# The stage ahead of the layers in written order: x loaded first, block steps pipelined, sort and first lists beside the last blocks

## The chip, the cores and the metric

The kernel runs on 1 core of one Trainium2 chip. The metric is device time in microseconds of one execution of the whole kernel, from launch to the last output. Beside it there is the trace of one profiled execution: the start and length of every instruction on each engine (PE is the TensorE matmul, PEld its weight load, DVE is VectorE, ACT is ScalarE, POOL is GpSimd, SP is SyncE, which here only issues DMAs) and of every DMA.

## The reference, cut to what matters

A graph of N = 3327 nodes is given by a matrix `adj` of int32 zeros and ones (about 16 neighbours a row), with features `x` of 3327 x 256 in float32. Layer 0 is a one-headed graph attention; the three layers after it are graph transformer layers with 8 heads, each node attending to its neighbours only.

```python
# layer 0
h = x @ Wt.T + bt                                     # 3327 x 64
s = leaky_relu(h @ Wa.T + ba, 0.2)                    # one score for each row
w = softmax(where(adj > 0, s, -9e15), axis=1)
y = x + (w @ h) @ Wp.T + bp
x = gamma * (y - mean(y)) * rsqrt(var(y) + 1e-5) + beta

# layers 1 to 3, weights of their own
q, k, v = split(layer_norm(x, g1, be1) @ w_qkv)       # 8 heads of 32
attn = softmax(where(adj != 0, q @ k.T * 32 ** -0.5, -inf))
x = x + (attn @ v) @ w_proj + b_proj
x = x + gelu(layer_norm(x, g2, be2) @ w1 + b1) @ w2 + b2   # w1 256 x 1024
```

As the score belongs to the row, all neighbours of a row get one weight and all others another; so layer 0 needs for each row the sum of `h` over the neighbours, the degree, and the sum of `h` over all nodes.

## The kernel before, in words

The nodes lie in `NB` = 26 blocks of 128 rows (the last has 127). There are two stages.

**The stage ahead of the layers (L172 to L468)** is layer 0 and all that the layers need. It stands in the scheduling of the tile framework: the program text says what depends on what, and the framework's scheduler sets the order of the instructions on each engine. In the order of the text:

- Small loads on ACT's queue: 15 columns of gains (`cols`, L188), the layer 0 weights `wt_raw`, `wp_raw` and a row of six vectors (L202), then `x` in 9 pieces (L209, L212) into `x0`, then `w_qkv` of layer 1 (`load_wq`, L90). The row is spread over the 128 partitions by matmuls with ones (L227).
- `h` (L258 to L274): per group of four blocks x is transposed on PE (L265), copied by DVE (L266), multiplied by Wt (`ph`, L270) and given its bias. When all of `h` is there, DVE splits it into three bf16 parts, `hs` (L279 to L283), with a column of ones behind them; 52 passes on PE sum `h` over all nodes (`phsum`, L288); L293 to L297 make the scores.
- The block loop (L401 to L432). Of a block: 1.66 MB of `adj` come on SP's queue into one of three `a32` buffers; ACT casts them to bf16 `abf` (L406); PE transposes its 26 tiles (L412) and ACT takes the sign of eight at a time into `aT` (L413); PE multiplies these with `hs` and sums into `pa` (L417), neighbour sums and degree together; ACT copies `pa` to `acc` (L424). For the neighbour lists DVE multiplies `abf` by column numbers (L421) and takes the eight largest of each of 13 segments of 256 columns (L423); the 104 candidates and the degree go to `node_dr` in DRAM (L426).
- After every fourth block: `count` (L304) makes the degree's one-hot `oh` and each node's rank among equal degrees, with matmuls; `finish` (L323) makes the softmax weights from the degree, mixes the sums, transposes (`nT`), multiplies with Wp (`pp`), adds to `x0`, and normalises: `moments` (L110: DVE statistics, then a power on POOL, L120), then on DVE L382 (subtract mean, times gamma) and L383 (times deviation, plus beta). Then a second norm for layer 1: statistics, `nmu` (DVE, L127), `xn` (ACT, L131), transposes and `hT` (ACT, L143), and `qkv_rows` (L157): k and v as `pk` (L161), q as `pq`, both copied by ACT, written on SP's queue to `kv_dr` and, with x, to `node_dr` (L388 to L391).
- Behind the loop the sort by degree (L435 to L468): the rank in all, from it one-hot matrices and 26 matmuls, and in the end `perm`, the node numbers sorted by degree.

**The layers (L471 to L781)** stand in an order written out by hand (`tc.manual_schedule()`, L779): each engine takes its instructions in the order in which the text issues them. Blocks are now 128 sorted nodes, in the order of `ORDER`. `node_rows` (L492) fetches a block's rows of `node_dr` with an indirect DMA of POOL by `perm`; `node_list` (L499) makes from the candidates the neighbours' numbers `idx`, the bias of empty places, and two counts (`found`), and ACT copies x to `x_sb`. Three blocks' rows are fetched ahead; the list of a block is made when the loop gets there. `gather` fetches k and v rows of up to four neighbours of each node with four indirect DMAs (L640, tiles `sl`); scores and weighted sums run on DVE (L651, L652, L684), the sums over neighbours on PE (L687), and `tail` (L546 to L589) does projection, norms, the feed-forward part, and k, v and q of the next layer. Layers 2 and 3 load their q rows on SP's queue (`load_q`); the `w_qkv` of the next layer is loaded at the start of each layer on ACT's queue (L90). A branch behind all, `general` (L812), computes the layers with full rows should a list not have held all neighbours; it is not entered with these inputs.

Of the kernel before, what the change touches and what calls it, by code (L numbers as in the profile page):

```python
# [36 lines left out]


# [11 lines left out]
NODES = 5  # L50
FH = FF // P // 2
# [6 lines left out]
def kernel(ctx: ExitStack, tc: tile.TileContext, ins, out: bass.AP):  # L58
# [21 lines left out]
    node_dr = dram.tile([NP, NODE], FP, name="node")  # L80
    q_dr = {L: dram.tile([P, NB, D], FP, name=f"q{L}") for L in LAYERS[1:]}
# [3 lines left out]
    pv = const.tile([P, 3, 16], FP, name="pv")  # L85
    wq_pool = ctx.enter_context(tc.tile_pool(name="wq", bufs=1))

    def load_wq(L):
        t = wq_pool.tile([P, 2, 3 * D], FP, tag="wq", name=f"wq{L}")
        nc.scalar.dma_start(t, wt(L, "w_qkv").rearrange("(c p) n -> p c n", p=P))  # L90
        return t


    brow = const.tile([6, D], FP, name="brow")
    for L in LAYERS:
        for k, name in enumerate(("b_proj", "b2")):
            r = 2 * (L - 1) + k
            nc.scalar.dma_start(brow[r:r + 1, :], wt(L, name)[None, :])
    b3 = const.tile([6, 3, D], BF, name="b3")
    for k in range(3):  # L100
        nc.vector.tensor_copy(b3[:, k, :], brow)
        if k < 2:
            nc.vector.tensor_sub(brow, brow, b3[:, k, :])
    bsum = const.tile([3, 6, D], BF, name="bsum")
    for k in range(3):
        nc.scalar.dma_start(bsum[k:k + 1, :, :], b3[:, k, :])
    ones3 = const.tile([3, P], BF, name="ones3")
    nc.vector.memset(ones3, 1.0)

# [60 lines left out]


    with ExitStack() as st:  # L172
# [4 lines left out]
        ps_g = st.enter_context(tc.tile_pool(name="ps_g", bufs=3, space=PSUM))  # L177
# [3 lines left out]

        cols = l0.tile([P, P], FP, name="cols")
        nc.vector.memset(cols, 0.0)
        for L in LAYERS:
            o = 16 * (L - 1)
            for k, name in ((0, "g1"), (2, "be1"), (4, "g2"), (6, "be2"), (8, "b1")):
                n = wt(L, name).shape[0] // P
                nc.scalar.dma_start(cols[o + k:o + k + n, :], wt(L, name).rearrange("(c p) -> c p", p=P))  # L188
        pt = big("pt_cols")
        nc.tensor.transpose(pt[:, :P], cols, ident)  # L190
        nc.vector.tensor_copy(pv, pt[:, :48].rearrange("p (l k) -> p l k", l=3))

        wt_raw = l0.tile([H0, D], FP, name="wt_raw")
        nc.scalar.dma_start(wt_raw, ins["L0_gnn_Wt"])
        wp_raw = l0.tile([P, 2, H0], FP, name="wp_raw")
        nc.scalar.dma_start(wp_raw, ins["L0_gnn_Wp"].rearrange("(c p) h -> p c h", p=P))
        nrow = 3 * D + 2 * H0 + 1
        row = l0.tile([1, nrow], FP, name="row")
        o = 0
        for name, n in (("gamma", D), ("beta", D), ("bp", D), ("bt", H0), ("Wa", H0), ("ba", 1)):  # L200
            src = ins[f"L0_gnn_{name}"]
            nc.scalar.dma_start(row[:, o:o + n], src if len(src.shape) == 2 else src[None, :])  # L202
            o += n

        x0 = l0.tile([P, NB, D], FP, name="x0")
        nc.vector.memset(x0[96:P, NB - 1, :], 0.0)
        for g, blocks in enumerate(GROUPS):
            full = [i for i in blocks if ROWS[i] == P]
            nc.scalar.dma_start(x0[:, full[0]:full[0] + len(full), :],  # L209
                                ins["x"][full[0] * P:(full[-1] + 1) * P, :].rearrange("(k p) d -> p k d", p=P))  # L210
        for p0, p1 in ((0, 112), (112, LAST)):
            nc.scalar.dma_start(x0[p0:p1, NB - 1, :], ins["x"][(NB - 1) * P + p0:(NB - 1) * P + p1, :])  # L212

        wtT = l0.tile([P, 2, H0], FP, name="wtT")
        wpT = l0.tile([H0, D], FP, name="wpT")
        for c in range(2):
            pt = big(f"pt_w{c}")
            nc.tensor.transpose(pt[:, :H0], wt_raw[:, c * P:(c + 1) * P], ident[:H0, :H0])
            nc.tensor.transpose(pt[:H0, P:2 * P], wp_raw[:, c, :], ident)
            nc.vector.tensor_copy(wtT[:, c, :], pt[:, :H0])  # L220
            nc.vector.tensor_copy(wpT[:, c * P:(c + 1) * P], pt[:H0, P:2 * P])

        rowb = l0.tile([P, nrow], FP, name="rowb")
        for c0 in range(0, nrow, 512):
            cw = min(512, nrow - c0)
            pb = big(f"pb_row{c0}")
            nc.tensor.matmul(pb[:, :cw], ones[0:1, :], row[:, c0:c0 + cw], start=True, stop=True)  # L227
            nc.scalar.copy(rowb[:, c0:c0 + cw], pb[:, :cw])
        gam_b, bet_b, bp_b = (rowb[:, k * D:(k + 1) * D] for k in range(3))
        bt_b = rowb[:, 3 * D:3 * D + H0]  # L230
        wa_b = rowb[:, 3 * D + H0:3 * D + 2 * H0]
        ba_b = rowb[:, nrow - 1:nrow]

# [21 lines left out]
        for s in range(1, SEGS):  # L255
            nc.gpsimd.tensor_copy(num[:, s, :], num[:, 0, :])

        h_sb = l0.tile([P, NB, H0], FP, name="h_sb")  # L258
        for g, blocks in enumerate(GROUPS):
            n = len(blocks)  # L260
# [43 lines left out]
        def count(g, acc):  # L304
# [8 lines left out]
            for j in range(n):  # L313
                nc.tensor.matmul(pc[:, j, :], tri, oh[:, b0 + j, :], start=True, stop=False)
                for m in range(j):
                    nc.tensor.matmul(pc[:, j, :], ones_bf, oh[:, b0 + m, :], start=False, stop=False)
# [655 lines left out]
```

## Time and profile before

| | |
|---|---|
| median of 4 runs | 3103.21 us (3098.36 to 3104.7) |
| profiled execution | 3107.19 us |
| its span, first to last instruction | 3105.4 us |
| mean granted TensorE clock | 0.741 of full speed |
| busy, share of the span | PE 58%, PEld 44%, DVE 57%, ACT 25%, POOL 47% |
| the stage ahead of the layers | from 0 to about 390 us |
| first instruction of x's loads | 24.49 us |
| last first-layer q row issued | 371.61 us |
| `perm` | 384.83 us |
| first gather of layer 1 | 397.12 us |

All times inside the trace count from the span's start. In a row of the order of time there stand: start, length, engine, line, operation, output <- inputs, shapes, how many like it follow in one go, and in brackets the idle time of the engine before it and whom it waited for. An engine name with q (ACTq, SPq) marks the issue of a DMA on that engine's queue; its length is the time to the landing. A table of stretches gives for each the length and the sum of the instructions' time on PE, PEld, DVE, ACT and POOL with their number, then the granted clock of PE, the share of time the DMA engines are busy, and GB/s.

### The profile page before, as it was taken

Reading aid. Unit: us, or ns where it says so; the run is one execution under the profiler, and the core shown is the slowest. Engines: PE = TensorE matmul, PEld = TensorE weight load, DVE = VectorE, ACT = ScalarE, POOL = GpSimd, SP = SyncE. Lnnn points to the kernel's source line nnn. Section 1 sums busy time; section 2 is a strip of 40 time slices with the busy share of each in tenths; the row PEclk is TensorE's granted clock in tenths of the full one; section 3 lists DMA queues with packets and bytes.
Section 4 is the critical chain, followed back from the end, with each engine's and each line's share of the span. In section 5 each row is a group of like instructions: output and inputs, shape, how many; then the busy total and the mean of one; then the engine's idle time right before and its main releaser. Section 6 shows DMA issues by size and latency. Waiting matters only on the chain. (4 is left out here: it accounts for less than half of the span.)

```text
span 3105.4 us, 25607 instructions
## 1 busy us (share of the span) xinstructions
PE 1793.7 (58%) x8349; PEld 1370.7 (44%) x8349; DVE 1778.1 (57%) x3203; ACT 768.0 (25%) x1420; POOL 1445.8 (47%) x1632
## 2 busy tenths in 40 slices
PE   6778405566655556825657665746634555445556
PEld 5555204444534444614445443435433444334445
DVE  4988546665556666426655655655264556554563
ACT  2877201222212122301322211211301212111112
POOL 0112164554555555254555655553354455555561
PEclk9999756777767777856878776767856777666767
DMA  5664164554545455164555555553354445544551
GB/s 189 210 216 163 67 195 124 145 158 131 162 144 150 140 157 149 51 208 116 149 155 146 162 162 149 153 158 100 122 157 136 118 135 158 162 142 142 147 154 29
DMA packets 154567, 451.22 MB, mean 145 GB/s; under 512 B 30575, under 2 KB 57849, under 8 KB 151097
## 3 DMA queue, kind: packets, MB, share of 16 engines
q0 software_dynamic: 111168, 363.51, 40.6%
q1 hardware_dynamic: 38462, 80.03, 7.6%
q10 hardware_dynamic: 4794, 5.94, 0.6%
q8 instruction: 69, 1.13, 0.2%
q14 instruction: 74, 0.61, 0.1%
HBM read 410.48 MB, written 38.88 MB: 145 GB/s over the span
## 5 line engine op out<-in xcount | busy, mean ns | idle before, releaser
L640 POOL DMA_INDIRECT sl<-kv,idx x1290 | 1233.2, 956 | 447.7 <-issue 373.7
L687 PE MATMUL po<-ident,sl 128*128 128x128 f32 x2580 | 492.4, 354 | 691.5 <-DVE sl L684 495.1
L687 PEld LDWEIGHTS po<-ident,sl 128*128 128x128 f32 x2580 | 411.7, 185 | 758.0 <-DVE sl L684 530.9
L651 DVE TENSOR_TENSOR sl<-sl,qp 128x1024 f32<-128x1024 f32 (+1 forms) x354 | 396.8, 1121 | 338.9 <-ACT qp L634 196.1
L580 PE MATMUL pd<-w,gT 128*128 128x256 f32 x1248 | 357.9, 447 | 217.8 <-ACT gT L571 157.8
L567 PE MATMUL pu<-fT,w 128*128 128x256 f32 (+1 forms) x1344 | 357.2, 410 | 120.0 <-issue 86.5
L652 DVE TENSOR_REDUCE sc<-sl 128x32 f32<-128x1024 f32 (+1 forms) x354 | 398.2, 1125 | 14.9 <-DVE sl L651 3.0
L580 PEld LDWEIGHTS pd<-w,gT 128*128 128x128 f32 x1248 | 276.1, 228 | 288.0 <-ACT gT L571 172.2
L684 DVE TENSOR_TENSOR sl<-sl,qp 128x1024 f32<-128x1024 f32 (+1 forms) x354 | 389.1, 1119 | 2.6
L567 PEld LDWEIGHTS pu<-fT,w 128*128 128x128 f32 x1344 | 265.4, 214 | 180.1 <-issue 109.9
L571 ACT ACTIVATE gT<-pu,pv 128x256 f32<-128x256 f32 (+1 forms) x336 | 135.1, 457 | 551.2 <-remote 316.5
L585 DVE TENSOR_TENSOR x_sb<-x_sb,pd 128x512 f32<-128x512 f32 (+1 forms) x42 | 27.3, 649 | 406.7 <-PE pd L580 394.0
L548 DVE TENSOR_TENSOR x_sb<-x_sb,pp 128x512 f32<-128x512 f32 (+1 forms) x42 | 27.3, 650 | 387.7 <-PE pp L546 365.3
L161 PE MATMUL pk<-wq,hT 128*128 128x512 f32 x312 | 193.8, 754 | 93.0 <-ACT hT L143 90.8
L120 POOL TENSOR_TENSOR rsig_f<-rsig_f,mhalf 128x2 f32<-128x2 f32 (+1 forms) x42 | 29.2, 695 | 305.9 <-DVE rsig_f L119 288.2
L602 POOL DMA_INDIRECT kv<-kvr,perm x52 | 52.4, 1007 | 240.4 <-ACT kvr L163 184.0
L693 ACT COPY oT<-po 128x256 f32<-128x256 f32 x78 | 29.1, 373 | 492.7 <-remote 252.7
L131 ACT ACTIVATE xn_f<-x_sb,nmu_f,rsig_f 128x256 f32<-128x256 f32 x78 | 43.4, 594 | 404.3 <-DVE nmu_f L127 258.5
L161 PEld LDWEIGHTS pk<-wq,hT 128*128 128x128 f32 x312 | 68.6, 239 | 153.0 <-ACT hT L143 99.3
L423 DVE MAX8 cand<-abf 128x8 f32<-128x256 bf16 x338 | 119.2, 412 | 0.0
L120 POOL TENSOR_TENSOR rsig_h<-rsig_h,mhalf 128x2 f32<-128x2 f32 (+1 forms) x28 | 19.5, 695 | 200.4 <-DVE rsig_h L119 200.4
L546 PE MATMUL pp<-w_proj,oT 128*128 128x256 f32 x312 | 95.7, 458 | 10.4 <-ACT oT L693 10.0
(217 smaller groups left out, 2021.7 us busy)
## 6 DMA issues: line engine op xcount, KB each, us to landing
a<-in_adj_dram SPq DMA_DIRECT2D x25, 1663.5 KB
sl<-kv,idx POOLq DMA_INDIRECT x1290
kv<-kvr SPq DMA_DIRECT2D x26, 256.0 KB
q<-qr SPq DMA_DIRECT2D x52, 128.0 KB
q<-q SPq DMA_DIRECT2D x52, 128.0 KB
w<-in_L_gnn_w_dram SPq DMA_DIRECT2D x6, 1024.0 KB
node<-x SPq DMA_DIRECT2D x26, 128.0 KB
node<-qr SPq DMA_DIRECT2D x26, 128.0 KB
```

The source lines that it names most:

```text
L161: nc.tensor.matmul(pk, hT[:, c, :], wq[:, c, D:], start=(c == 0), stop=(c == 1))
L423: nc.vector.max(out=cand[:, 8 * m:8 * m + 8], in_=ab3[:, m, :])
L546: nc.tensor.matmul(pp[:, j, :], oT[:, c, j * P:(j + 1) * P], w["w_proj"][:, c, :], start=False, stop=(c == 1 and j == n - 1))
L567: nc.tensor.matmul(pu[:, a, :n * P], w["w1"][:, c, f * P:(f + 1) * P], fT[:, c, :n * P], start=(c == 0), stop=(c == 1))
L571: nc.scalar.activation(gT[:, f0 + a, :n * P], pu[:, a, :n * P], AF.Gelu_apprx_tanh, bias=pv[:, L - 1, 8 + f:9 + f])
L580: nc.tensor.matmul(pd[:, j, :], gT[:, f, j * P:(j + 1) * P], w["w2"][:, h * FH + f, :], start=False, stop=(h == 1 and f == FH - 1 and j == ...
L602: nc.gpsimd.indirect_dma_start(out=kv_dr[L + 1][:, :], out_offset=bass.IndirectOffsetOnAxis(ap=perm[:, b:b + 1], axis=0), in_=kv, in_offse ...
L640: nc.gpsimd.indirect_dma_start(out=t[:, k - a, :], out_offset=None, in_=kv_dr[self.L][:, :], in_offset=bass.IndirectOffsetOnAxis(ap=idx[:, ...
L651: nc.vector.tensor_mul(kq, kq, self.qp[:, None, :D].to_broadcast([P, n, D]))
L652: nc.vector.tensor_reduce(self.sc[:, a:z, :], kq.rearrange("p s (h d) -> p s h d", h=HEADS), AX.X, ALU.add)
L684: nc.vector.tensor_mul(vv, vv, self.pw[:, a:z, :, None].to_broadcast([P, n, HEADS, HD]))
L687: nc.tensor.matmul(self.po[:, c, :], t[:, k, D + c * P:D + (c + 1) * P], ident, is_transpose=True, start=False, stop=(a + k == self.S - 1 ...
```

## The change

It rewrites the stage ahead of the layers, and keeps what it computes. The whole stage now stands in `tc.manual_schedule()`, so that every engine takes its instructions in the order of the text.

- *Loads.* On ACT's queue only the layer 0 weights and the row; on SP's queue x first, then three blocks of `adj`, then the columns, biases and `w_qkv`. `load_wq` issues on SP's queue in all layers.
- *h.* In 13 pairs of blocks instead of 7 groups; the copy of the transposed x moves from DVE to ACT; the split into three parts is made per two pairs, beside the following ones. The casts of blocks 0 and 1 come at the end of this.
- *Block loop.* Iteration i issues, in turns of up to eight tiles, transposes and signs of block i and the sums `pa` of block i-1; then the copies and writes of block i-1, the cast of block i+2 and the load of block i+4; one step of `finish`; the candidates of block i; one step of `finish` again (two of them in the last three blocks).
- *finish* is a generator which takes in `count`; each `yield` is a step's end. Several groups can be under way, each of them moved by a step at a time. The groups are `FIN`: five of four blocks, then 3, 2 and 1. The first norm is computed by ACT (x times deviation, minus mean times deviation) and by POOL (times gamma, plus beta, two blocks at a time).
- *Sort and first lists.* `order` is a generator too, started behind the last group's first step. It ends with the lists of the first three sorted blocks (`EARLY`), whose candidates come with `node_cand` from a table of their own, `cand_dr`; so each candidate row is written twice. `idx`, `bias`, `found` and the list's scratch tiles move to a pool that lives through both stages, and `segb` is filled at the start.
- *Layer 1* fetches the whole rows of the first three blocks (`node_rows`), copies their x, and makes lists from the fourth block on.

The diff, cut to its core:

```diff
+FIN = [list(range(a, z)) for a, z in ((0, 4), (4, 8), (8, 12), (12, 16), (16, 20), (20, 23), (23, 25), (25, 26))]
+EARLY = 3
...
+    cand_dr = dram.tile([NP, CAND + 1], FP, name="cand")
+    lists = ctx.enter_context(tc.tile_pool(name="lists", bufs=1))
...
     def load_wq(L):
-        nc.scalar.dma_start(t, wt(L, "w_qkv").rearrange("(c p) n -> p c n", p=P))
+        nc.sync.dma_start(t, wt(L, "w_qkv").rearrange("(c p) n -> p c n", p=P))
...
+    def node_cand(b):
+        nodes_[b] = lists.tile([P, NODE], FP, tag="node", bufs=NODES, name=f"node_{b}")
+        nc.gpsimd.indirect_dma_start(
+            out=nodes_[b][:, 2 * D:], out_offset=None, in_=cand_dr[:, :],
+            in_offset=bass.IndirectOffsetOnAxis(ap=perm[:, b:b + 1], axis=0))
...
-    with ExitStack() as st:
+    with ExitStack() as st, tc.manual_schedule():
-        ps_g = st.enter_context(tc.tile_pool(name="ps_g", bufs=3, space=PSUM))
+        ps_g = st.enter_context(tc.tile_pool(name="ps_g", bufs=4, space=PSUM))
+        nc.scalar.dma_start(wt_raw, ins["L0_gnn_Wt"])
+        nc.scalar.dma_start(wp_raw, ins["L0_gnn_Wp"].rearrange("(c p) h -> p c h", p=P))
...
+            nc.scalar.dma_start(row[:, o:o + n], src if len(src.shape) == 2 else src[None, :])
...
+            nc.sync.dma_start(x0[:, full[0]:full[0] + len(full), :],
+                              ins["x"][full[0] * P:(full[-1] + 1) * P, :].rearrange("(k p) d -> p k d", p=P))
...
+        load(0)
+        load(1)
+        load(2)
...
+        def x_turned(m):
+            xTs[m] = l0w.tile([P, 2, 2 * P], FP, tag="hT0", name=f"xT_{m}")
+            pb = big(f"px_{m}").rearrange("p (c r) -> p c r", c=2)
+            for j, i in enumerate(PAIRS[m]):
+                for c in range(2):
+                    nc.tensor.transpose(pb[:, c, j * P:(j + 1) * P], x0[:, i, c * P:(c + 1) * P], ident)
+            nc.scalar.copy(xTs[m], pb)
...
+        for m in range(len(PAIRS)):
+            x_turned(m)
+            if m:
+                h_rows(m - 1)
+        cast(0)
+        h_rows(len(PAIRS) - 1)
+        cast(1)
+        load(3)
...
+        def finish(f):
...
+            nc.scalar.activation(m1, m1, AF.Exp)
+            nc.scalar.activation(m0, m0, AF.Exp)
...
+            yield
...
+            yield
...
+            yield
+            pps = []
             for j0 in range(0, n, 2):
...
+                pps.append((j0, m, ps))
+            for j0, m, ps in pps:
                 xi = x0[:, b0 + j0:b0 + j0 + m, :]
                 nc.vector.tensor_add(xi, xi, ps[:, :m, :])
                 nc.gpsimd.tensor_add(xi, xi, bp_b[:, None, :].to_broadcast([P, m, D]))
+            yield
             views = [x0[:, i, :] for i in blocks]
+            mv, rs = moments(views, f"l0_{f}")
+            yield
+            nm = small.tile([P, 4], FP, tag="nmu", name=f"nm0_{f}")
+            nc.vector.scalar_tensor_tensor(nm[:, :n], mv[:, :n, 0], -1.0, rs[:, :n], ALU.mult, ALU.mult)
             for j, xi in enumerate(views):
-                nc.vector.scalar_tensor_tensor(xi, xi, mv[:, j, 0:1], gam_b, ALU.subtract, ALU.mult)
-                nc.vector.scalar_tensor_tensor(xi, xi, rs[:, j:j + 1], bet_b, ALU.mult, ALU.add)
+                nc.scalar.activation(xi, xi, AF.Identity, bias=nm[:, j:j + 1], scale=rs[:, j:j + 1])
+            for j0 in range(0, n, 2):
...
+                nc.gpsimd.tensor_tensor(xi, xi, gam_b[:, None, :].to_broadcast([P, m, D]), ALU.mult)
+                nc.gpsimd.tensor_add(xi, xi, bet_b[:, None, :].to_broadcast([P, m, D]))
+            yield
+            yield
+            mv, rs = moments(views, f"q1_{f}")
...
+            yield
+            for j0 in range(0, n, 2):
+                js = slice(j0, min(j0 + 2, n))
+                xns = normed(l0w, views[js], mv[:, js, :], rs[:, js], f"q1_{f}_{j0}")
+                yield
+                hT = l0w.tile([P, 2, 2 * P], FP, tag="hT0", name=f"hT0_{f}_{j0}")
+                turned(big, hT, xns, *gains(1, 0), f"q1_{f}_{j0}")
+                yield
+                for j in range(len(xns)):
+                    i = b0 + j0 + j
+                    kv, q = qkv_rows(l0w, big, wq1, hT[:, :, j * P:(j + 1) * P], 1, f"1_{i}")
...
+                    yield
+        def order():
...
+            for b in ORDER[:EARLY]:
+                node_cand(b)
+            yield
+            yield
+            for b in ORDER[:EARLY]:
+                node_list(b)
+                yield
+        def steps(k):
+            for _ in range(k):
+                for e in list(under):
+                    if next(e, 0) == 0:
+                        under.remove(e)
...
+        for i in range(NB + 1):
...
             for k0 in range(0, NB, 8):
                 kn = min(8, NB - k0)
+                if i < NB:
...
+                    nc.scalar.activation(aTs[i][:, k0:k0 + kn, :], pt[:, :kn, :], AF.Sign)
+                if i:
+                    for k in range(k0, k0 + kn):
+                        nc.tensor.matmul(pa[:, :3 * H0 + 1], aTs[i - 1][:, k, :], hs[:, k, :],
+                                         start=(k == 0), stop=(k == NB - 1))
...
+            if i:
...
+                nc.scalar.copy(accs[f][:, j, :], pa[:, :3 * H0 + 1])
+                cand = cands.pop(i - 1)
+                nc.scalar.copy(cand[:, CAND:], accs[f][:, j, 3 * H0:])
+                nc.sync.dma_start(cand_dr[(i - 1) * P:i * P, :], cand)
+                nc.sync.dma_start(node_dr[(i - 1) * P:i * P, 2 * D:], cand)
+            if i + 2 < NB:
+                cast(i + 2)
+                if i + 4 < NB:
+                    load(i + 4)
+            if i == NB:
+                break
+            steps(1)
+            ab3 = abfs.pop(i).rearrange("p (s c) -> p s c", s=SEGS)
             nc.vector.tensor_mul(ab3, ab3, num)
...
             for m in range(SEGS):
                 nc.vector.max(out=cand[:, 8 * m:8 * m + 8], in_=ab3[:, m, :])
+            if i and i - 1 in last_of:
+                under.append(finish(last_of[i - 1]))
+            steps(2 if i >= NB - 3 else 1)
+        under.append(finish(last_of[NB - 1]))
+        steps(1)
+        under.append(order())
+        while under:
+            steps(1)
...
             if first:
-                for b in ORDER[:NODES - 2]:
+                for b in ORDER[:EARLY]:
                     node_rows(b)
-                node_list(ORDER[0])
+                    node_x(b)
...
-                        for m in ((1, 2) if k == 0 else (k + 2,)):
-                            if m < NB:
-                                node_list(ORDER[m])
+                        if EARLY <= k + 2 < NB:
+                            node_list(ORDER[k + 2])
+                            node_x(ORDER[k + 2])
```

## The prediction

> **What bounds the kernel now.** I read the busy table of five stretches first, then the order of time at the marks between them, then one period of the block loop. The stretches (busy us of each engine, granted clock, DMA share, GB/s):
>
> ```profile
> 0.00:25.00 25.00, 1.64 (x6) 0.81 (x6) 4.01 (x21) 0.00 (x0) 5.61 (x25) 1.00 0.60 211
> 25.00:50.00 25.00, 22.88 (x96) 19.06 (x97) 7.38 (x15) 10.85 (x6) 0.00 (x0) 1.00 0.99 367
> 75.00:325.00 250.00, 189.53 (x1618) 145.02 (x1615) 222.13 (x677) 193.34 (x269) 44.84 (x70) 0.93 0.55 185
> 325.00:400.00 75.00, 27.30 (x101) 15.23 (x101) 36.48 (x124) 14.23 (x34) 14.27 (x80) 0.64 0.30 105
> ```
>
> The order is PE, PEld, DVE, ACT, POOL. For 25 us nothing computes. In the loop over the adjacency blocks DVE is 89% busy, and ACT and PE 77% and 76%: three engines near their limit. Then 75 us in which none is half busy. These are the three places the change can touch; the layers after them keep their code almost unchanged. The marks, in order of time (start, length, engine):
>
> ```profile
> 24.49 5.73 ACTq L209 DMA_DIRECT2D x<-in_x_dram  x7
> 65.80 1.30 ACT L413 ACTIVATE aT<-pt 128x1024 bf16<-128x1024 bf16 x2 [0.24 <-PE pt L412]
> ...
> 322.00 0.32 ACT L424 COPY acc<-pa 128x193 f32<-128x193 f32 x1 [2.70 <-PE pa L417]
> 371.61 0.39 SPq L390 DMA_DIRECT2D node<-qr  x1
> 384.83 0.18 DVE L468 CAST perm<-permf 128x26 uint32<-128x26 f32 x1
> 388.22 1.21 POOL L496 DMA_INDIRECT node<-node,perm  x1 [0.82 <-DMA w_proj<-in_L_gnn_w_proj_dram]
> 397.12 0.95 POOL L640 DMA_INDIRECT sl<-kv,idx  x1 [3.94 <-DVE found L522]
> ```
>
> x is asked for only at 24.5; block 0's signs run from 65.8; the last block's sums are copied at 322.0; the last rows leave at 371.6, then sort (to 385), node rows and first list, and layer 1's first gather at 397.1. So start 65.8, loop 256.2, tail 75.1 us. One period of the loop (four blocks and one `finish`):
>
> ```profile
> 206.60 1.78 ACT L131 ACTIVATE xn_q<-x,nmu_q,rsig_q 128x256 f32<-128x256 f32 x3 [3.03 <-DVE nmu_q L127]
> 209.08 2.95 PE L161 MATMUL pk<-wq,hT 128*128 128x512 f32 x4
> 216.71 1.88 PE L161 MATMUL pk<-wq,hT 128*128 128x512 f32 x4
> 250.96 1.78 ACT L131 ACTIVATE xn_q<-x,nmu_q,rsig_q 128x256 f32<-128x256 f32 x3 [3.03 <-DVE nmu_q L127]
> 208.00:211.00 3.00, 3.00 (x7) 1.20 (x7) 3.00 (x6) 2.90 (x6) 0.10 (x1) 0.50 0.07 18
> ```
>
> The same work returns after 44.36 us, or 11.1 per block. And a warning: PE waited 2.9 us before 207.25, its granted clock in 208 to 211 is 0.50, and the same four matmul passes take 2.95 instead of 1.88.
>
> **Start.** Eight small loads and x now go first. Loads land about 2 us after issue here (wt_raw issued 21.37, used 23.55), two of them wait for an earlier one, so the row is in at 6.5 and its broadcast (L227, 0.85 a pass) ends at 8.3. Then 13 pairs of blocks: 4 transposes and 8 `ph` passes take 0.87 + 1.75 = 2.6 us at the pace of 35 to 45, and 0.48 + 0.94 = 1.4 at the pace after 50. In before, the pace changes at 50.0, when PE has been dense for 17.5 us and when the loads end. Both put the change in after at about 26 (8.3 + 17.5; or 9.3 MB at 400 GB/s plus 2). So 6.8 slow and 6.2 fast pairs, 34.8; `phsum` 52 passes in 6 us, 41; first transposes, signs at **42**: 23.8 us gained. All fast gives 34, all slow 55. The 6.3 us of h splitting that lay on DVE after h (60.8 to 71) now run group by group beside PE.
>
> The Trainium skill, "TensorE: Matmul & The Clock Gate", Part 1 (the HAM clock gate), says that some 3.4 us of sustained work open the clock, and that an idle window of as much closes it to half. Its first half disagrees with this trace (dense from 32.5, slow until 50); by it the start would be about 35 and the sum below 7 us lower. Its second half fits the 2.95 us row and speaks against this change, since the new order leaves PE longer waits.
>
> **Loop.** Now every engine takes its instructions as written, and I read them in the built program's order. Per block: signs 3.13, acc and cand 0.35 to 0.5, cast 2.9 on ACT; L421 1.84 and 13 L423 at 0.33, 6.13 together, on DVE; on PE 8 transposes 0.5 and 8 `pa` 0.7. `finish` has 16 steps, two per block, one before L421 and one after the L423s, so two groups overlap. The moved L382/L383 take some 0.40 off DVE eight times per group and put four ACT normalisations (2.1 us) and four POOL passes (1.28 each, as L378) in place. By work alone ACT and DVE need 36 us per four blocks. But in order they wait for each other. From one block's first sign to the next's, with the trace's durations:
>
> 1. A group enters. The older group's second moments wait for the POOL passes; L421 starts at 4.05, the maxima end at 10.2, then `nmu`, then the new group's dc, oh and 12 small dependent operations (0.2 each where dependent) before ACT gets its exponentials: 2.35 more, 0.2 for them. **13.05**, where ACT had 8.4 us of work.
> 2. ACT's hT stands behind the cast, so it ends at 7.6; only then can PE do this step's k, v and q (1.88 and 1.0, or 2.95 and 1.0 after its 4 us wait), then ACT copies them, PE transposes hn, ACT copies nT. 11.6 warm, with cold passes **13.1**.
> 3. DVE's first work is adding `pp`, which on PE stands behind the transposes, `pa` (3.25) and a k, v, q row (2.6). The adds end at 8.5, L421 and maxima at 14.7, `nmu` 14.9, and ACT's xn (1.1) needs that: **16.1**. This is the worst: DVE idles some 8 us.
> 4. Like 2 without nT, with normalisations: 11.1, and after PE's 6.7 us wait in step 3 **12.4**.
>
> Sum **54.7** against 44.36. Blocks 0 to 3 (no `finish` yet) run at 6.2 to 6.6 each, limited by L421 and maxima; blocks 4 to 8 take 12.1, 7.1, 6.6, 11.1, 15.4 as the pipe fills. So the ninth block's signs start at 42 + 78.5 = 120.5; three periods, 284.6; blocks 21 to 24 at 13.1, 16.1, 13.2, 10.5, and 17 to the last copy: 354.5. The loop takes 312.5, which is **56.3 more**. Bounds of the period: 48 (every wait of PE warm, dependent small operations at 0.1, half of step 3 hidden) to 58 (cold in every step); 4.6 periods' worth, so -31 to +15 us.
>
> **Tail.** After the last copy the last group needs eleven rounds of steps, with two older groups and the sort between; by the same chaining 42 us to the last q copy (the order's 10 us of DVE work lie inside; cover gone, they cost 14, as 371 to 385 does now). The write lands 2.4 later, 53 POOL memsets (1.9) wait for it, then four node rows (1.25 each) stand before the first gather, whose index is ready: 51.3, **23.8 less**. In order of doubt: 8 us either way. The second write of each candidate row (26 more DMAs on SP) lies behind the casts; two of SP's eight outstanding places are the price, and I take 0, up to 5.
>
> **Layer boundary.** The next w_qkv load moves from ACT's queue to SP's, ahead of the first q load. At layer 2 DVE waits for that q: issued 1337.1, used 1349.96. At 12.8 us for the 2.5 MB before it, 0.79 MB more is 0 (the bytes compete anyway) to 4; I take **2**. Layer 1 loses two lists from its first turn, which lie beside gathers now: 0, at most -2.
>
> Sum: -23.8 + 56.3 - 23.8 + 2 = **+10.7**. The profiled execution took 3107.19 (span 3105.4), 4 above the median of the runs; it would become 3118, and the median 3103.21 becomes **3114**.
>
> **The rivals.** (a) The order costs little: waits of step 3 and of the cold passes are mostly absorbed, because ACT and DVE need only 36 of 44 us. From a period of 50.4 down (54.7 less 20 us over 4.6 periods) the change is faster by over 0.2%; at 48 to 50 it gives 3083 to 3092, and at the present 44.4 some 3067. For it: gains at both ends rest on marks seen above. Against: the built order shows the adds ahead of L421. 0.27. (b) It comes out even, 3097 to 3109.4 (0.2%, about what a measurement of this kernel can tell from no change): period near 52. 0.18. (c) Slower than forecast: PE, busy 33 us of 55, falls to the clock of the layers (0.75) throughout, period 60 and a longer tail: 3140 to 3150. 0.10. (d) The forecast, 3109.4 to 3140: 0.45. It would also be wrong in doing nothing if x were not what the start waits for, but L265's wait names x's DMA.
>
> **How the numbers follow.** Slower 0.45 + 0.10 = 0.55; same 0.18; faster 0.27. The range 3084 to 3142 takes the loop's bounds and 8 us of the tail; beyond it I leave 0.2. The forecast's own range is 3109 to 3140.
>
> **What would show it.** First steady signs at about 42; the fourth-block period of L131's pairs at 54.7, with PE's granted clock under 0.9 in the loop; in every fourth block DVE idle some 8 us with `pp` as releaser, ahead of the x add; ACT waiting for DVE's `nmu` and for pk; the last acc copy near 354, the first gather near 406, 9 us later than now; q at layer 2 used 2 us later after its issue. A period under 50 or a first gather before 391 would prove me wrong on the loop; signs after 50, on the start.

## The result and the profile after

| | before | after |
|---|---|---|
| median of the runs | 3102.14 us (57 runs) | 3112.0 us (36 runs) |
| ratio after / before | | 1.0033 [1.0024, 1.0043] |
| profiled execution, span | 3107.19, 3105.4 us | 3106.77, 3105.0 us |

The change makes the kernel 9.9 us slower on the medians; the forecast was 10.7. The single profiled execution of after is as short as that of before, within the scatter of single runs (3097 to 3128), so the traces are read stage by stage, and the sum is judged on the medians. (In rows with a q, as SPq, the length is that of the issuing instruction and not, as said above, the time to the landing: the prediction itself counts 2.4 us to the landing of a q row, whose issue has a length of 0.39.) Five stretches of after, the first four those shown of before, the last exactly three periods of the loop (length, then PE, PEld, DVE, ACT, POOL busy, clock, DMA share, GB/s):

```profile
0.00:25.00 25.00, 18.31 (x74) 15.19 (x75) 7.88 (x32) 5.87 (x9) 6.13 (x38) 1.00 0.88 317
25.00:50.00 25.00, 22.06 (x220) 21.26 (x219) 19.95 (x51) 18.17 (x18) 0.00 (x0) 1.00 0.53 200
75.00:325.00 250.00, 158.20 (x1262) 125.38 (x1261) 177.92 (x513) 163.33 (x223) 63.59 (x75) 0.79 0.50 162
325.00:400.00 75.00, 53.55 (x279) 34.51 (x279) 59.25 (x188) 32.30 (x71) 27.99 (x30) 0.76 0.19 65
124.00:288.00 164.00, 109.34 (x823) 83.44 (x822) 111.76 (x321) 109.27 (x154) 38.73 (x49) 0.81 0.51 166
```

The empty start is filled: PE works 18 of the first 25 us, where it worked 1.6. (The clock of 1.00 in the first row stands for no record of it: the trace's first record lies at 25.83 us.) The loop has lost its density: DVE was busy 222 of the same 250 us and is now busy 178, at a granted clock of 0.79 instead of 0.93. The marks, in order of time:

```profile
41.88 3.13 ACT L587 ACTIVATE aT<-pt 128x1024 bf16<-128x1024 bf16 x4 [0.23 <-PE pt L586]
364.55 0.32 ACT L600 COPY acc<-pa 128x193 f32<-128x193 f32 x1 [1.50 <-PE pa L590]
410.77 0.37 ACT L178 COPY qr<-pq 128x256 f32<-128x256 f32 x1 [0.32 <-PE pq L176]
420.76 0.94 POOL L758 DMA_INDIRECT sl<-kv,idx  x1 [0.30 <-issue]
```

| mark (us) | before | forecast | after |
|---|---|---|---|
| block 0's signs | 65.8 | 42 | 41.9 |
| last copy to `acc` | 322.0 | 354.5 | 364.6 |
| first gather of layer 1 | 397.1 | 405.8 | 420.8 |

The start is as forecast, the loop and the tail are worse than forecast, and the first gather is 23.6 us late instead of 8.7. Less than half of that reaches the median.

What the loop lost is seen in the waits of DVE and ACT between 75 and 325 us (who <- for whom: total us, times, longest):

```profile
DVE x L470 <- PE pp L466: 43.7, 10, 10.2
...
ACT xn_q L141 <- DVE nmu_q L137: 41.3, 8, 7.6
```

DVE stands before the additions of `pp` in five groups, 8.7 us for each on average, and ACT stands before its normalisation, which waits for DVE's `nmu`, as long again. That is the forecast's chain of step 3. The period, from ACT's first normalisation in one group to that in the next, is 54.63 us here:

```profile
206.99 1.09 ACT L141 ACTIVATE xn_q<-x,nmu_q,rsig_q 128x256 f32<-128x256 f32 x2 [7.59 <-DVE nmu_q L137]
261.62 1.09 ACT L141 ACTIVATE xn_q<-x,nmu_q,rsig_q 128x256 f32<-128x256 f32 x2 [7.60 <-DVE nmu_q L137]
```

### The profile page after: what moved, and what is told of

Read it like the earlier page. It is cut to its first block, busy times and chain, and to the rows that moved or that the text cites. A ratio compares the mean times of both kernels' runs of the same rounds, so it can differ in the third digit from the quotient of the medians.

```text
span 3105.0 us, 25704 instructions
## 1 busy us (share of the span) xinstructions
PE 1798.8 (58%) x8346; PEld 1379.2 (44%) x8346; DVE 1784.6 (57%) x3214; ACT 792.1 (26%) x1464; POOL 1489.4 (48%) x1666
## 5 line engine op out<-in xcount | busy, mean ns | idle before, releaser
L171 PE MATMUL pk<-wq,hT 128*128 128x512 f32 x312 | 201.4, 780 | 124.8 <-ACT hT L153 122.6
L176 PEld LDWEIGHTS pq<-wq,hT 128*128 128x128 f32 x312 | 69.3, 223 | 68.1 <-issue 46.9
```

The source lines that it names most:

```text
L171: nc.tensor.matmul(pk, hT[:, c, :], wq[:, c, D:], start=(c == 0), stop=(c == 1))
L176: nc.tensor.matmul(pq[:, :D], hT[:, c, :], wq[:, c, :D], start=(c == 0), stop=(c == 1))
```

## The experiments

Each ratio is against the kernel before in the same comparison, from five rounds. There were three comparisons, each on a chip of its own (14, 3 and 11); the median of before was 3074.05, 2481.58 and 3096.45 us in them. On the second chip the same program ran 600 us faster; where in the kernel that lies is taken up with its runs.

**x_first.** The kernel before, scheduled as it was, with only the loads turned round: layer 0's weights first on ACT's queue, x first on SP's, the columns and bias rows on SP behind it, and their transpose and splits behind h's split:

```diff
-            nc.scalar.dma_start(x0[:, full[0]:full[0] + len(full), :],
+            nc.sync.dma_start(x0[:, full[0]:full[0] + len(full), :],
...
-                nc.scalar.dma_start(cols[o + k:o + k + n, :], wt(L, name).rearrange("(c p) -> c p", p=P))
...
+                nc.sync.dma_start(cols[o + k:o + k + n, :], wt(L, name).rearrange("(c p) -> c p", p=P))
```

> The kernel before, with one thing changed: the layer 0 weights and the row go first on ACT's queue and x first on SP's, and the columns and biases behind x; the scheduler keeps the order of all the rest. Main theory (x's late load holds the start, and nothing else does): first steady signs at 42 to 46 instead of 65.8, the period of four blocks stays at 44.4, so first gather about 375 and the time 20 to 24 us under before, near 3080. Rival (the loop is bound by DVE from its start, and DVE still has 6 us of splits and the scores behind h): the loop stretches at its head, first gather about 385, gain about 10.

Measured: 3055.08, ratio 0.9935 [0.9912, 0.9958], 20 us faster. Signs at 39.3 instead of 65.8, last copy at 293.9 instead of 322.0, first gather at 368.3 instead of 397.1. The earlier start goes through loop and tail undiminished; 20 of the 28.8 us are left at the end. So the loads are a gain by themselves, and the rest of the change loses more than that.

**sched.** The changed kernel, with the stage left to the framework's scheduler; the layers keep their written order:

```diff
-    with ExitStack() as st, tc.manual_schedule():
+    with ExitStack() as st:
```

> The changed kernel with the manual schedule of the stage ahead of the layers taken away: same text, same loads, same steps, same work on each engine, but the scheduler orders each engine's instructions. Main theory (the written order costs the loop, by waits of one engine behind another): period of four blocks 44 to 46 instead of 54.65, last acc copy about 315 instead of 364.6, first gather 365 to 380 instead of 420.8, time 3065 to 3085. Rival (the work itself has become slower: normalisation over ACT and POOL, candidates written twice, loads on one queue): period above 50, time above 3095.

Measured: 3014.88, ratio 0.9804 [0.9782, 0.9826]: 59 us faster than before, where after is slower. The first gather comes at 338.7. Four blocks take 40.7 us (mean over blocks 9 to 21), where after takes 54.7 and before 42.5 (the 44.36 shown ahead was one period; none of the sum's terms rests on it). Three periods of sched, to be held against the last row of the first table:

```profile
99.00:221.00 122.00, 97.68 (x828) 75.24 (x826) 109.42 (x344) 109.83 (x159) 42.22 (x54) 0.94 0.76 258
```

DVE and ACT do the same work in both, 109 to 112 us; it is spread over 164 us in the written order and over 122 us in the scheduler's. Here ACT and DVE are both 90% busy. The waits of its loop (75 to 277 us):

```profile
DVE x L470 <- PE pp L466: 1.1, 2, 1.0
...
ACT xn_q L141 <- DVE nmu_q L137: 6.1, 4, 2.6
```

43.7 us have become 1.1 and 41.3 have become 6.1. How, DVE's order of time in sched shows:

```profile
161.30 1.87 DVE L614 TENSOR_TENSOR abf<-abf,num 128x3328 bf16<-128x3328 bf16 x1
163.20 1.08 DVE L617 MAX8 cand<-abf 128x8 f32<-128x256 bf16 x3
164.20 1.45 DVE L470 TENSOR_TENSOR x<-x,pp 128x512 f32<-128x512 f32 x2
165.56 3.36 DVE L617 MAX8 cand<-abf 128x8 f32<-128x256 bf16 x10
```

The scheduler has put the two additions in the middle of a block's maxima, at a point where `pp` is there. In after the same two stand ahead of L614 and hold it up:

```profile
253.30 0.69 DVE L470 TENSOR_TENSOR x<-x,pp 128x512 f32<-128x512 f32 x1 [9.95 <-PE pp L466]
...
254.77 2.33 DVE L614 TENSOR_TENSOR abf<-abf,num 128x3328 bf16<-128x3328 bf16 x1
```

**adds_late.** The changed kernel in written order, with one more step boundary in `finish`, so that the additions fall behind the maxima of a block instead of ahead of L614 (every later step moves on by half a block):

```diff
                 pps.append((j0, m, ps))
+            yield
             for j0, m, ps in pps:
```

> The changed kernel with one more step end in finish, between the pp matmuls and the x adds; so the adds come behind a block's maxima instead of ahead of its multiplication, and all later steps change places. Main theory (the x adds waiting for pp, ahead of the candidates' multiplication, make the worst of the four iterations): the 16.2 us iteration falls to 12 or 13 and the period from 54.65 to about 50 or 51, which over 4.6 periods is 17 to 20 us less, near 3093. Rival (other steps then wait in the same way, as all steps change their place): period 54 to 56, time within 6 us of the changed kernel's 3112.

Measured: 3076.47, ratio 1.0007 [0.9991, 1.0023]: no difference from before that these runs can show. The period is 48.5, the four iterations 11.5, 14.1, 11.0 and 11.3 us instead of 13.4, 11.9, 13.1 and 16.2. The 16.2 is gone; a 14.1 is new, where DVE's multiplication (L615 in this kernel) waits 4.1 to 5.0 us for PE's `pt`. The last copy comes 23 us earlier than in after (341.6), the first gather only 15 (405.7): a group now has one step more, and the chain behind the last block is 8 us longer. One `yield` takes the change's loss away, within the interval, but it moves a wait as well as removing one.

**dve_norm.** Written order kept, the first norm put back on DVE for all groups, so that ACT and POOL lose the added work:

```diff
-                nc.scalar.activation(xi, xi, AF.Identity, bias=nm[:, j:j + 1], scale=rs[:, j:j + 1])
...
-                nc.gpsimd.tensor_tensor(xi, xi, gam_b[:, None, :].to_broadcast([P, m, D]), ALU.mult)
-                nc.gpsimd.tensor_add(xi, xi, bet_b[:, None, :].to_broadcast([P, m, D]))
+                nc.vector.scalar_tensor_tensor(xi, xi, mv[:, j, 0:1], gam_b, ALU.subtract, ALU.mult)
+                nc.vector.scalar_tensor_tensor(xi, xi, rs[:, j:j + 1], bet_b, ALU.mult, ALU.add)
```

> The changed kernel with the first norm back on DVE (two passes for each block, as before) in place of ACT and POOL. Theory of the prediction (the written order's waits set the period, not this work): the 3.2 us more on DVE fall into its idle time, the wait for the POOL passes ahead of the second moments goes, so the period is 53 to 54.7 instead of 54.65, time within 8 us of after_b. Rival (DVE is the bound, the move off it paid): period 57 to 58, time 13 to 16 us over after_b.

Measured: 3109.92, ratio 1.0029 [1.0007, 1.0050], beside after's 1.0053 [1.0031, 1.0074] in the same comparison; the intervals overlap. The period is 54.64 against 54.5, the four iterations 13.5, 12.1, 13.1, 16.2. DVE has 3.1 us more to do in a group (121.1 us busy in three periods, 111.8 in after), ACT and POOL have their added operations less, and the loop does not notice: its length is set by the order, not by what the engines have to do.

**lists_back.** Written order kept; the early lists and the second write of each candidate row taken out, three lists made in layer 1 as before:

```diff
-            for b in ORDER[:EARLY]:
-                node_cand(b)
...
-                nc.sync.dma_start(cand_dr[(i - 1) * P:i * P, :], cand)
...
+                node_list(ORDER[0])
```

> The changed kernel without the early lists: no candidate table of its own, one write of each candidate row, and the first three lists made in layer 1 as before. Tells apart why the layers take 14 us less than before (whole time +9.9, first gather +23.6). If the early lists are it: first gather 2 to 6 us earlier than 420.8 by less work ahead of it, or later by the 4 us of the first list, but the layers longer by 10 or more, time 3115 to 3125. If it is something else (queue of the weight load, place of the tiles, chance of one profile): layers as in the changed kernel, time 3106 to 3114.

Measured: 3094.25, ratio 1.0071 [1.0049, 1.0094]. The period is 54.6, so the 26 additional writes cost the loop nothing. From the last copy to the first gather it takes 60.4 us instead of 56.2: the early lists are worth 4.2 us. Its start happened to be 3.5 us later (45.4), of which below. Its first 100 gathers in layer 1 take 196.2 us, after's 195.6, before's 200.9: the lists made early are not what shortens layer 1.

**after_again, pause, late_w.** The second comparison asks whether the layers give back what the stage loses. after_again is the unaltered kernel after. pause keeps DVE from handing over `perm` until eight large memsets are done, in layer 1 ahead of the first node rows, which moves the first gather by 46.3 us and nothing else of the layers. late_w loads the layers' weights behind the first gathers' issue instead of ahead of them, so that the q load of layer 2 has nothing before it. The edits of pause and of late_w:

```diff
+                for _ in range(8):
+                    nc.vector.memset(x_sb, 0.0)
+                nc.vector.tensor_copy(perm, pf)
```

```diff
-            w = load_weights(L)
-            wqn = load_wq(L + 1) if L < LAYERS[-1] else None
+            w = wqn = None
...
+                    if w is None:
+                        w = load_weights(L)
+                        wqn = load_wq(L + 1) if L < LAYERS[-1] else None
```

> The changed kernel once more, unaltered, beside the kernel before on the same chip: a second profile of it. The first gather stood 23.6 us later than before, the whole time only 9.9. If the layers really give back 14 us: ratio 1.002 to 1.005 again, and from the first gather to the end about 10 to 20 us under the other kernels of this call at equal layer code. If the one profile was a short one by chance: ratio 1.006 to 1.008, and layers as in the others.

> The changed kernel with idle time put in behind the stage: at the start of layer 1 DVE fills x_sb eight times and writes perm again, so the node rows and the first gather wait for it while nothing else runs. Its length is read from the profile (an estimate of 30 to 50 us). Theory A (the layers take their time whenever they start): time over the changed kernel's rises by the whole shift of the first gather, within 4 us. Theory B (a later start is partly given back, as a rested PE is granted a higher clock in the layers): it rises by at least 10 us less, with a higher granted clock in the first 100 gathers than 0.64.

> The changed kernel with each layer's weight loads (2.5 MB, and the next w_qkv) issued behind the first gathers instead of ahead of the first q loads. Tests the boundary term of the prediction: the first q row waits behind these bytes. Theory (the wait for q is queueing behind the weights): from a layer's first gather to the first q copy 5 to 7 us instead of 16.3 (layer 2) and 11.4 (layer 3), each boundary 4 to 9 us shorter, also the last rows' landing ahead of layer 1; time 10 to 20 us under the changed kernel. Rival (the gathers' data is what the first scores wait for anyway, or the first tail then waits for w_proj): within 4 us of the changed kernel.

Measured: after_again 2506.68, ratio 1.0103 [1.0078, 1.0128]; pause 2551.43, 1.0280 [1.0256, 1.0305]; late_w 2502.24, 1.0087 [1.0065, 1.0109].

Here before took 2481.58, after 25.1 more: as much as the first gather's delay (420.5 against before's 397.1, which is from the first comparison's trace). The pause costs 44.7 us for 46.3. Nothing is given back. late_w is within its interval of after_again, and its first gather is 3.8 us earlier (416.7) from an earlier start; both have a second layer of 688.2 us, though what starts it differs (second layer's first gather, and DVE's first score, of after_again and then of late_w):

```profile
1148.72 0.98 POOL L758 DMA_INDIRECT sl<-kv,idx  x1 [2.58 <-issue]
1165.21 0.95 DVE L769 TENSOR_TENSOR sl<-sl,qp 128x768 f32<-128x768 f32 x1 [25.72 <-ACT qp L752]
```

```profile
1144.73 0.98 POOL L758 DMA_INDIRECT sl<-kv,idx  x1 [2.54 <-issue]
1153.96 0.95 DVE L769 TENSOR_TENSOR sl<-sl,qp 128x768 f32<-128x768 f32 x1 [18.49 <-DMA sl<-kv,idx]
```

With q early the first score stands 9.2 us behind the first gather instead of 16.5, and the layer is no shorter. So where the layers are short, the q load is not on the path that ends last, and a q that comes some us later for `w_qkv` on SP's queue costs nothing that these runs can show.

The 600 us between the comparisons lie in the layers: the stage's marks of after_again agree with those of after within 0.3 us, and the layers take 2079.5 instead of 2684.2. PE's waits in the layers show what is different, first after, then after_again:

```profile
PE po L805 <- DVE sl L802: 566.4, 115, 37.0
...
PE pu L685 <- issue: 103.0, 69, 13.3
PE po L805 <- issue: 97.1, 57, 17.6
```

```profile
PE po L805 <- DVE sl L802: 597.4, 175, 35.3
PE pu L685 <- ACT fT L153: 38.0, 18, 3.1
```

In after PE stands idle for hundreds of us with nothing that the profile shows to wait for ("issue"), between single matmuls of one feed-forward part:

```profile
931.72 0.59 PE L685 MATMUL pu<-fT,w 128*128 128x256 f32 x1 [1.74 <-issue]
933.82 0.59 PE L685 MATMUL pu<-fT,w 128*128 128x256 f32 x1 [1.52 <-issue]
```

These rows sum to 281 us in after's layers and 305 in before's (from 425 us on); in the four traces of the second comparison they come to 0.2 us at most. In after's stage ahead of the layers PE has none. ACT too stands there with no releaser that the profile names ("issue" or "remote"): 1136 us in after's layers, 14 in after_again's. What the engines lack there is not shown, and the chip and the comparison changed together.

**after_b, pause_b.** The unaltered after, and the pause, again where the layers are long:

> The changed kernel unaltered, a third time, as the measure for pause_b on the same chip. In the second of these comparisons the layers took 600 us less than in the first, on both kernels, and PE never starved in them; there the whole time rose by as much as the first gather (ratio 1.0103, +25 us for +23.4). If the layers show single matmuls at 2.1 us each again: ratio 1.001 to 1.006, so part of the 23.6 us is taken back; if they do not: 1.008 to 1.012.

> The pause of some 46 us ahead of layer 1 again. In the other comparison it cost 44.8 us for 46.3 of shift, all of it. Theory A (a later start always costs its full length): 43 to 48 us over after_b here too. Theory B (where PE starves in the layers, a later start is partly taken back): 10 us less or more, 25 to 36.

Measured: after_b 3115.98, ratio 1.0053 [1.0031, 1.0074]; pause_b 3151.17, 1.0168 [1.0138, 1.0198]. The first gathers come at 420.8 and 465.1. The pause's 44.4 us cost 35.2, or, with both intervals, some 24 to 47. That leans to a part being given back in long layers, and does not settle it.

**best1, best1_b.** sched, with late_w's edit and the first norm of the last three groups on DVE as in before; once in the second and once in the third comparison:

```diff
-    with ExitStack() as st, tc.manual_schedule():
+    with ExitStack() as st:
...
+            if f < len(FIN) - 3:
...
+            else:
+                for j, xi in enumerate(views):
+                    nc.vector.scalar_tensor_tensor(xi, xi, mv[:, j, 0:1], gam_b, ALU.subtract, ALU.mult)
+                    nc.vector.scalar_tensor_tensor(xi, xi, rs[:, j:j + 1], bet_b, ALU.mult, ALU.add)
```

> The scheduled form of the changed kernel (0.9804 of before, -59 us) with two more edits: weight loads behind the first gathers as in late_w, and the first norm of the last three groups on DVE (as before), where DVE idles and the way over ACT and POOL is a chain. Theory: the last q row leaves at about 320 instead of 328.6, as its buffer no longer waits for a write that stands behind 2 MB of weights, first gather 326 to 332, boundaries 4 to 9 us shorter each, ratio 0.971 to 0.977. Rival (the tail is bound by the chain of steps, the boundaries by the gathers): 0.979 to 0.981.

> The scheduled form with late weight loads and the last norms on DVE, a second time. It gained 58 us (0.9765) where the scheduled form alone gained 59 (0.9804) in the other comparison; so the two small edits brought nothing that shows. Expected: 55 to 62 us under before here, whatever the level of the layers.

Measured: 2422.91, ratio 0.9765 [0.9741, 0.9790], and 3032.76, 0.9775 [0.9745, 0.9806]. The first gather comes at 341.4 and 338.0, beside 338.7 in sched. That is 58 and 70 us, the second more than the 55 to 62 expected. The two additional edits moved nothing that can be told from sched's own gain. It beats both kernels, by about 2.3% of before and, in the same two comparisons, 2.7 to 3.3% of after.

## Why the prediction was right, and where it was not

The total was right within 0.8 us, and the sign rests on what was forecast: a written order in which DVE waits ahead of L614. But two terms were mis-sized in one direction, and what the layers take, which the sum held fixed, went the other way.

**Start: right.** 23.9 us gained, forecast 23.8. Part of the hit is luck. The pairs of `h` began at 11.3 and not at 8.3, as the four broadcast passes ran from 8.0 to 11.4; they were faster than priced, 2.45 and 1.3 us where the sum had 2.6 and 1.4. And the same loads and matmuls gave signs between 38.2 and 45.4 us in the runs of the written order, since the moment at which PE's pace changes moved.

**Period: right, mostly by its own steps.** From block 9's signs to block 21's, three periods, it is 164.2 us (forecast 164.1). The four iterations measured 13.4, 11.9, 13.1 and 16.2 where steps 4, 1, 2 and 3 had 12.4, 13.05, 13.1 and 16.1: steps 2 and 3 as forecast, the other two off by 1.0 and 1.2 in opposite directions, and that these cancel is luck. DVE idles 8.7 us a group for `pp`, 9.95 in the one shown (forecast 8). The clock in the loop is 0.81 (forecast under 0.9). sched, adds_late and dve_norm together show that the cause is this order: the same work in another order takes 40.7, one boundary moved takes 48.5, other work in the same order 54.6.

The rule weighed there, the Trainium skill, "TensorE: Matmul & The Clock Gate", Part 1 (the HAM clock gate), is borne out in its second half. Four passes behind a wait of 3.75 us, a little more than the page's window, with PE's clock at 1.00 before it:

```profile
241.05 3.57 PE L171 MATMUL pk<-wq,hT 128*128 128x512 f32 x4 [3.75 <-ACT hT L153]
```

The stretch that they fill has a granted clock of 0.50:

```profile
241.00:244.00 3.00, 2.95 (x4) 1.40 (x5) 2.35 (x8) 0.45 (x1) 0.10 (x1) 0.50 0.87 342
```

They take 3.57 us where the warm ones take 1.88; behind step 3's wait of 7.2 us it is 3.78. The prediction priced them at 2.95, from a row of before that was cold in part only (the clock is 0.66 from 209 to 212). Before's tail has a wholly cold one, which shows the right price, 0.6 to 0.8 more for each:

```profile
363.32 3.78 PE L161 MATMUL pk<-wq,hT 128*128 128x512 f32 x4 [0.66 <-ACT hT L143]
```

**Loop: +66.5 where the sum had +56.3; fill and drain were mis-sized.** The fill to the ninth block is 3.4 us longer (first signs at 123.8, forecast 120.5). The drain is 6.7 longer: blocks 21 to 24 take 13.1, 16.2, 17.3 and 14.2 where the sum had 13.1, 16.1, 13.2 and 10.5, and the last 15.8 for 17. From block 23 on two steps stand behind the maxima of a block, and the next block's signs stand behind two rows of k, v, q on PE and ACT; the prediction gave these blocks 13.2 and 10.5 us. And a zeroing of the last block on POOL was not in the sum at all:

```profile
319.75 2.87 POOL L268 MEMSET abf<- 32x3328 bf16 x1
322.65 2.97 ACT L269 CAST abf<-a 127x3327 bf16<-127x3327 int32 x1 [0.94 <-POOL abf L268]
326.13 3.70 PE L171 MATMUL pk<-wq,hT 128*128 128x512 f32 x4 [4.15 <-ACT hT L153]
```

It holds the last cast up by 0.94, and that in turn ACT's next hT. The passes are cold, but the clock was at 0.50 already from 316 on.

**Tail: -18.9 where the sum had -23.8.** From the last copy to the last q copy it takes 46.2, forecast 42; two of its k and v passes are cold (3.78 and 3.65). From there to the first gather 10.0, forecast 9.3. The mechanism holds: sort and first lists lie beside the last groups. The place with most doubt was given 8 us either way, and was off by 5. (The range's lower end, 3084, leaves these 8 us out: with them the prediction's own terms give 3075.)

**Boundary and layers: +2 forecast, about -14 on the medians.** This is the step that failed. The first q of layer 2 does come later after its issue, by 3.2 us (16.1 where before had 12.9, forecast 2):

```profile
1366.28 0.38 ACT L752 COPY qp<-q 128x256 f32<-128x256 f32 x1 [18.77 <-DMA q<-q]
```

But late_w, where the layers are short, shows no price for it in the time. The second write of the candidates costs 0 (lists_back's period), as was taken. What failed is the assumption that the layers take as long as before once they start. Of 23.6 us of delay at the first gather 9.9 were left here, about 16 to 20 in after_b, and all where the layers are short. The shift of the first gather against before's 397.1, beside the time gained or lost:

| | first gather | time | with interval |
|---|---|---|---|
| after | +23.6 | +10 | +7 to +13 |
| x_first | -28.8 | -20 | -27 to -13 |
| sched | -58.4 | -60 | -67 to -53 |
| adds_late | +8.6 | +2 | -3 to +7 |
| lists_back | +31.7 | +22 | +15 to +29 |
| after_b | +23.7 | +16 | +10 to +23 |
| pause_b | +68.0 | +52 | +43 to +61 |
| dve_norm | +24.2 | +9 | +2 to +15 |
| best1_b | -59.2 | -70 | -79 to -60 |
| after_again | +23.4 | +26 | +19 to +32 |
| pause | +69.7 | +69 | +63 to +76 |
| late_w | +19.6 | +22 | +16 to +27 |
| best1 | -55.7 | -58 | -64 to -52 |

(The time is the ratio less 1, times before's median; before's first gather is one trace's, so each shift carries its scatter too.) In the four lowest rows, where PE stands 0.2 us at most without a releaser, shift and time agree; above, the changed kernels come out 2 to 16 us better than their first gather, x_first 9 worse. x_first has the layers of before, so 9 us can be scatter; and best1_b comes out 11 better with an earlier first gather, so it is not simply a later start that is given back. It is not the early lists, since lists_back gives back as much. Whether a later start is absorbed by the stalls, or the stalls fall otherwise in another program, no run here tells apart: that stays open. So the forecast's total was right because the loop's and the tail's 15 us too little were met by some 16 us that nothing in the prediction foresaw: that it lies within 0.8 us is luck. In the comparison without the stalls the change costs 25.1 us, which lies inside the forecast's own range too (+6 to +37).

**The rivals.** (a), the waits absorbed, is refuted for the written order (period 54.7, not under 50.4); its idea that ACT and DVE have room is right, as sched shows. (b) needed a period near 52: refuted. (c), PE at the layers' clock throughout with a period of 60, is refuted: PE's clock fell to 0.81, and the period held.

## What to carry to other kernels

An order written by hand makes every wait of an engine a wait for all that stands behind it: before moving a step, look for the instruction whose input comes from the far end of another engine's queue, and put it behind independent work, as the scheduler put two additions between a block's maxima. Gains of a bundle should be tried apart: here the loads first and the pipelined steps were worth 60 us, and the order that came with them put the first gather 82 us back. And a forecast made of a start, a period, a fill, a drain and a tail should price the fill and drain by their own instructions, since that is where the steps change.

## What the runs showed of the hardware

PE's pace on dense work changes at no fixed time. In after, eight `ph` passes go from 1.81 to 1.00 us at about 25.5, with PE busy without a break since 8.0:

```profile
23.08 1.81 PE L353 MATMUL ph<-wtT,xT 128*128 128x64 f32 x8
26.96 1.00 PE L353 MATMUL ph<-wtT,xT 128*128 128x64 f32 x8
```

The first record of the granted clock in this trace lies at 25.83 us, and says 1.00; the 1.00 in tables of earlier stretches is no record. In sched the pace changes at about 18.3 and the first record lies at 18.4, in lists_back both come at about 33, in before at about 50 and at 50.6. So the change of pace is most likely the clock granted in full, though no record shows the clock before it. In after, sched and lists_back it came 10 to 25 us after PE's work became dense, while their loads all end at about 27: neither of the two reasons that the prediction gave, 17.5 us of density or the loads' end, sets it, and a start priced by it carries some 4 us either way.

One program took 2500 us on one chip and 3110 on another, with a stage of equal length on both: in the layers, stalls of PE without a releaser are there by hundreds of us, or not at all. A difference of 10 us in the former is best checked in the latter, where the time follows the first gather to within the interval.
